# A two-layer attention and expert kernel: the first keys, the early jobs' transposes and the last gates are put in another order

## The chip, the cores and the metric

The kernel runs on one core of a Trainium2 chip. The metric is the device time of one execution in microseconds (us), lower is better. In what follows TensorE is called PE, VectorE DVE, ScalarE ACT, GpSimd POOL, and SyncE, which only starts DMAs here, SP. Each of these engines works through its own list of instructions in a fixed order, and an instruction that waits for another engine holds up everything behind it on its own list.

## The reference

Eight batches of 512 tokens with 256 features pass through two blocks. Each block is a layer norm, a cross-attention onto 64 context rows, and a feed-forward part, all with residuals.

```python
x = x + xattn0(layernorm(x), ctx)     # 16 heads of 16, 64 keys for each batch, biases on q, k, v, o
x = x + ffn0(layernorm(x))            # top 384 of 512 tokens: gelu(x @ w_block); the others pass through
x = x + xattn1(layernorm(x), ctx)     # the same with a mask
x = x + moe(x)                        # 8 experts, top 2 by softmax gate, weights made to sum to 1
                                      # expert: (silu(x @ g.T) * (x @ u.T)) @ down.T, 1024 hidden
```

Everything is float32. Layer norm has no learned scale. The expert part works on all 4096 tokens, each sent to two experts.

## The kernel before, in words

**Tiles.** A batch is four tiles of 128 tokens. Its residual rows stay in on-chip memory (`x_sb`). The context of all batches lies transposed in `ctxT`, so one pair of products with `wk` makes the keys of eight batches: `keys(l, c)` (L319 to L336) computes half c of layer l's keys and writes them twice, masked for the two heads of a pair by `headm`, into `kbd` (two DVE instructions at L332 for each half). `batch_values(b)` (L338 to L355) does the values of batch b for both layers and adds the bias `pre_b` while writing `vbd` (two DVE instructions at L353).

**The front stage.** For every batch a chain of steps is built: layer norm (statistics L385, `rstd` by POOL L390, `shift` L396, `xn` on ACT L399), transposes to `ps_x` (L414), queries (L446), scores `sc` (L476), the row maximum (L483), its transposes `pm` (L491), the transposed scores `st`, the context, the output product, then the ranked feed-forward part, the second attention, and the routing. Routing ends with `xr`, a token's row beside its expert and weight, which POOL scatters by indirect DMA into the table `xs` in device memory (L816). When half of the batches are scattered, seven "early" expert jobs of 256 tokens run between the steps of the other half (`early_steps`, L1066 to L1178): `enter` transposes the job's rows (L1111) and copies them on ACT (L1114), four `gates` steps do the gate and up products (L1135), and `down(0)` and `down(1)` do two output products (L1162), which POOL scatters with adding. Their weights come from SP in pieces of a single buffer set.

**The order.** The steps are laid out by a string, `ORDER` (L50 to L59). Each character takes the next step of one chain: a digit for a batch, A to H for the ranking of a batch, k for keys, v for `batch_values`, s for setups sorted by a number, l for the two lists of jobs, j for early jobs. `in_order` makes every step's instructions follow those of the step before it on PE, DVE, ACT and POOL. So the string is the order of the engines' queues in the front stage. DMAs on SP are not in it, but stand in program order with the ties named in the code.

**The late jobs.** After the front stage come 18 full jobs, 7 single and 11 paired ones, in the loop at L1443 to L1483. `load` (L1256) fetches a job's rows `xg` (L1277) and weights `wgu` (L1300), `wdn` on SP into four sets. `enter` (L1309) transposes the rows (L1317, ACT copy L1319), `gate_up_full` (L1340) makes the hidden rows (L1349), and `down` (L1396) the outputs, which POOL adds to `out_dram` (L106). A job's rows need every scatter of the front stage (`routed`). For the very first late job `load` issues the weights ahead of the rows (`late`), and its `enter` stands behind the last early job's outputs.

**Start.** `wk0`, half of batch 0's rows, `bk0`, `wv0` and `bq0` are on ACT's DMA queue, the context, the other rows and the remaining weights on SP's, and only the two value biases `bv0`, `bv1` on POOL's.

Of the kernel before, what the change touches and what calls it, by code (L numbers as in the profile page):

```python
# [8 lines left out]
F32 = mybir.dt.float32  # L9
I32 = mybir.dt.int32  # L10
# [37 lines left out]
NQ = P // QR  # L48

ORDER = """  # L50
sssssss0s0ksk0s1020001s0k110s1vs0s031010s7s2s40v320v2410030v20120ss01040502A010A30A0As10
1013010343201130005s12010sk0112151761Bs2B1BB112120241201v102s2050223s022302412C22123C2C0
21C02131012110323150030sv024110331231041025231052000043313234260000D14D34Ds14D2341v23361
3421632333442123454126154343114325134311114432E2524E1111544E452356E547224342372523465352
64345645256352452222F36F35F63F222246455635547335546357453674356647435356733333556646v7l6
3333476G464jj77j5jGj666j5j7jj47Gjjj765j7457j4G5j64654j7j6556747j5j7644644444j76sH6jj5644
44j557j76j7j57jj7Hsj76jjjjHH7565j65jj676jj7jj6j57j5j6j75557j5555jj7j6j667j55557jjjs67j66
j76j7676j66j76s66667j7jjjj7jj6666j77j7j7jjjjj77jjs7j7j7j7j7j777jj77jjjljj77jj77jj
"""  # L59


# [1 line left out]
def xattn_ffn_kernel(ctx: ExitStack, tc: tile.TileContext, a: dict, out: bass.AP):  # L63
# [28 lines left out]
    def after(i, others):  # L92
        for other in others:
            tc.add_manual_dep(
                i, other.name,
                mybir.DependencyInfo(mybir.DependencyClass.Sync, mybir.DependencyReason.DATA),
                reason="rows that it needs",
            )

    def apart(i, others, reason):  # L100
        for other in others:
            tc.declare_no_dep(i, other, reason=reason)
# [14 lines left out]
    with ExitStack() as front:  # L117
# [36 lines left out]
        def load_layer(l, names, q):  # L154
            for n in names:
                how = load_mat if n[0] == "w" else load_col if n in ("bk", "bq") else load_row
                layers[l][n] = how(q, f"{n}{l}")


        ctxT = pre[:, 0, :].rearrange("p (c b k) -> p c b k", c=2 * NC, b=B)[:, 0:NC]  # L160
        for c in range(NC):
            nc.sync.dma_start(
                ctxT[:, c].rearrange("p b k -> p (b k)"), a["ctxT"][c * P : (c + 1) * P, :]
            )
        load_layer(0, ("wk",), nc.scalar)
        for t in range(TB):
            q = (nc.scalar, nc.scalar, nc.sync, nc.sync)[t]
            q.dma_start(x_sb[:, t, :], x_t[0][:, t, :])
        load_layer(0, ("bk", "wv", "bq"), nc.scalar)
        load_layer(1, ("wv",), nc.sync)  # L170
        load_layer(0, ("wq", "bo", "wo"), nc.sync)
        nc.sync.dma_start(x_sb[:, TB : 2 * TB, :], x_t[1])
        load_layer(1, ("wk", "bk"), nc.sync)
        for b in range(2, 4):
            nc.sync.dma_start(x_sb[:, b * TB : (b + 1) * TB, :], x_t[b])
# [40 lines left out]
        def within(at, name, shape, bounds, lasts=False):  # L216
# [14 lines left out]
        every = slice(0, P)  # L231
        mhalf = const.tile([P, TB], F32, name="mhalf")
        setups.append((-0.9, lambda: nc.gpsimd.memset(mhalf, -0.5)))
        setups.append((
            -0.855, lambda: [load_layer(l, ("bv",), nc.gpsimd) for l in range(2)]
        ))

        ownh = within(
            -0.88, "ownh", [HC],
# [60 lines left out]
        mxs = []  # L300
        for i in range(3):
            mx = const.tile([P, TB, P], F32, name=f"mx{i}")
            setups.append(((-0.86, 0.25, 0.5)[i], lambda mx=mx: nc.vector.memset(mx, 0.0)))
            mxs.append(mx)
        turn = [0]

# [4 lines left out]
        vbd = const.tile([P, 2, B, NG, 2, DK], F32, name="vbd")  # L313
        for l in range(2):
            layers[l]["vbd"] = vbd[:, l]
        setups.append((
            -0.93, lambda: (nc.vector.memset(vbd[:, 0], 0.0), nc.gpsimd.memset(vbd[:, 1], 0.0)),
        ))

        def keys(l, c):  # L320
            w = layers[l]
# [727 lines left out]
        def part_of_room(*shape):  # L1049
            n = 1  # L1050
            for k in shape:
                n *= k
            v = room[:, took[0] : took[0] + n]
            took[0] += n
            names = " ".join("abc"[: len(shape)])
            return v.rearrange(f"p ({names}) -> p {names}", **dict(zip("abc", shape)))
# [2 lines left out]
        e_xg = part_of_room(2, RW)  # L1059
        e_xT = part_of_room(NC, 2, P)  # L1060
        e_sg = [part_of_room(1, 2 * P)]
        e_now = keep.tile([P, 2, D], F32, name="e_now")
        e_w = {}
        piece = 2 * P

# [118 lines left out]
        for b in range(B):  # L1184
# [2 lines left out]
                attention_steps(b, 0, layers[0], False) + ffn  # L1187
                + attention_steps(b, 2, layers[1], True) + route_steps(b)
            )
        chains["k"] = [lambda l=l, c=c: keys(l, c) for l in range(2) for c in range(NC)]  # L1190
        chains["v"] = [lambda b=b: batch_values(b) for b in range(B)]
        chains["s"] = [step for _, step in sorted(setups, key=lambda p: p[0])]
        chains["l"] = [early_list, full_list]
        chains["j"] = early = []
        jobs_steps = [early_steps(j) for j in range(NEARLY)]
        early += jobs_steps[0][0]
        for j, (_, steps) in enumerate(jobs_steps):

            loads = list(jobs_steps[j + 1][0]) if j + 1 < NEARLY else []
            for n, step in enumerate(steps):  # L1200
                early.append(step)
                if loads and n != len(steps) - 2:
                    early.append(loads.pop(0))


        engines = (
# [46 lines left out]
    def kind(j):  # L1253
        return "full" if j < NLATE else "one" if j < NLATE + NONE else "pair"

    def load(j, late=False):  # L1256

        what = kind(j)
        subs, n = (2 if what == "full" else 1), (2 if what == "pair" else 1)
        first = j if what != "pair" else NLATE + NONE + 2 * (j - NLATE - NONE)  # L1260
        size = P if what != "pair" else P // 2

        with tc.issue_after(last.pop().ins) if last else nullcontext():
            at = [
                (
                    nc.sync.value_load(
                        jobs[0:1, 0, u : u + 1], min_val=0, max_val=E * QROWS + P - subs * size
                    ),
                    nc.sync.value_load(jobs[0:1, 1, u : u + 1], min_val=0, max_val=E - 1),
                )  # L1270
                for u in range(first, first + n)
            ]
        xg = moe.tile([P, 2, RW], F32, tag="xg", name=f"xg_{j}", bufs=3)

        def rows():
            for u, (row, _) in enumerate(at):
                i = nc.sync.dma_start(  # L1277
                    xg[u * size : u * size + size, 0:subs, :],
                    xs[bass.ds(row, subs * size), :].rearrange("(s p) w -> p s w", p=size),
                ).ins  # L1280

                if what == "pair":
                    after(i, tail_sent)
                else:
                    for other in tail_sent:
                        tc.declare_no_dep(i, other, reason="rows of tokens alone")
                    after(i, routed)

        if not late:
            rows()  # L1290
        w = []
        for u in range(n):
            pool = wpool[sets[0] % 4]
            sets[0] += 1
            wgu = pool.tile([P, NC, 2 * FF], F32, tag="wgu", name=f"wgu_{j}_{u}")
            wdn = pool.tile([P, NF, D], F32, tag="wdn", name=f"wdn_{j}_{u}")
            w.append((wgu, wdn))
        for (_, e), (wgu, _) in zip(at, w):
            for c in range(NC):
                nc.sync.dma_start(  # L1300
                    wgu[:, c, :], gu_t[bass.ds(e, 1), :, c, :].rearrange("e p o -> (e p) o")
                )
        if late:
            rows()
        for (_, e), (_, wdn) in zip(at, w):
            i = nc.sync.dma_start(wdn, dn_t[bass.ds(e, 1), :, :, :].rearrange("e p f o -> (e p) f o"))
        last.append(i)
        return xg, w
# [127 lines left out]
    assert sorted(order) == [j for j in range(NJOB) if j != spare]  # L1436

    def load_at(i):
        return load(order[i], i == 0) if i < len(order) else None

    loads = [load_at(0), load_at(1)]
    entered = []
    in_order(lambda: entered.append(enter(order[0], loads[0][0])))  # L1443

    def placed(i, step):

        if i < NPIN:
            got = []
            in_order(lambda: got.append(step()))
            return got[0]  # L1450
        return step()

    pending = None
    for i, j in enumerate(order):
        w = loads.pop(0)[1]
        xT, tok, wt = entered.pop(0)
        if i > 0:
            loads.append(load_at(i + 2))
        if i == 0:

            hT = placed(i, lambda: gate_up_full(j, xT, w, None, range(NF // 2)))
            entered.append(placed(i, lambda: enter(order[1], loads[0][0])))
            placed(i, lambda: gate_up_full(j, xT, w, hT, range(NF // 2, NF)))
        elif j < NLATE:
            hT = placed(i, lambda: gate_up_full(j, xT, w))
        else:
            h, hT = placed(i, lambda: gate_up_rows(j, xT, w))
        if i == 0:
            small_list()
            unit_list()  # L1470
            loads.append(load_at(2))
        if 0 < i < len(order) - 1:
            entered.append(placed(i, lambda: enter(order[i + 1], loads[0][0])))
        if pending is not None:
            placed(i, lambda: down(*pending))
        if j >= NLATE:
            placed(i, lambda: turn(j, h, hT))
        pending = (j, hT, w, tok, wt)
# [55 lines left out]
```

## Time and profile before

| what | value |
|---|---|
| time, median of 3 runs | 1164.99 us (1164.78 to 1166.47) |
| profiled execution, its own time | 1173.17 us |
| profiled execution, span from first to last instruction | 1171.5 us |
| mean granted PE clock in it | 0.998 of full |
| PE busy | 1146.6 us, 98% of the span |
| DVE / ACT / POOL busy | 574.6 / 372.9 / 283.5 us |
| data moved by DMA | 203.53 MB |

The time of a run is that of the whole execution; the span counts from the core's first to its last instruction in the profile. All durations below come from the one profiled execution, which took 8.2 us more than the median of the runs. In rows of the timeline the first number is the start in us from the span's start, the second the time to the end of the group, then engine, line, operation, result and operands, shape, and in brackets how long the engine had been idle before and what ended the wait.

### The profile page before, as it was taken

How to read it: one execution, taken by the hardware profiler on the slowest of the kernel's cores; microseconds unless marked ns; L12 is line 12 of the kernel's file. 1: busy time of each engine (PE TensorE's matmuls, PEld its weight loads, DVE VectorE, ACT ScalarE, POOL GpSimd, SP SyncE). 2: the span in 40 equal slices, each digit the busy share in tenths (PEclk: the TensorE clock that was granted, in tenths of full speed). 3: DMA queues.
4: the chain of work that ended last, by engine and by line, in shares of the span. 5: the costliest groups of instructions: out<-in, count | busy, mean ns of one | idle time of the engine just before them, and what ended most of it. 6: DMA issues, size and time to landing. Idle time of an engine off the chain costs nothing. (4 is left out here: it accounts for less than half of the span.)

```text
span 1171.5 us, 20900 instructions
## 1 busy us (share of the span) xinstructions
PE 1146.6 (98%) x8010; PEld 825.0 (70%) x8010; DVE 574.6 (49%) x1664; ACT 372.9 (32%) x713; POOL 283.5 (24%) x307
## 2 busy tenths in 40 slices
PE   7999999999999999999999999999999999999997
PEld 3565666656657777778787876777767777677786
DVE  6898888878878676556722221221212222222211
ACT  3655645645543433232121121221111211112210
POOL 5331134123440411431412112112121121211212
PEclk9999999999999999999999999999999999999999
DMA  9000001010125344445789688896889967987711
GB/s 270 2 1 2 1 20 38 19 56 20 38 86 165 105 138 115 136 145 163 207 329 353 237 295 293 303 312 224 288 290 330 312 214 272 314 309 237 279 14 19
DMA packets 119988, 203.53 MB, mean 174 GB/s; under 512 B 10608, under 2 KB 105712, under 8 KB 108368
## 3 DMA queue, kind: packets, MB, share of 16 engines
q1 hardware_dynamic: 100048, 179.35, 43.5%
q0 software_dynamic: 14496, 17.86, 7.5%
q10 hardware_dynamic: 5344, 4.98, 1.3%
q8 instruction: 64, 1.05, 0.4%
q14 instruction: 36, 0.29, 0.1%
HBM read 180.38 MB, written 23.47 MB: 174 GB/s over the span
## 5 line engine op out<-in xcount | busy, mean ns | idle before, releaser
L1349 PE MATMUL gu<-xjT,wgu 128*128 128x256 f32 x1152 | 252.0, 379 | 0.7 <-ACT xjT L1319 0.7
L1349 PEld LDWEIGHTS gu<-xjT,wgu 128*128 128x128 f32 x1152 | 217.6, 190 | 31.0 <-issue 1.2
L106 POOL DMA_INDIRECT out_dram<-now,tok x63 | 98.5, 1564 | 474.6 <-DVE now L1414 296.4
L1406 PE MATMUL o<-wdn,hT 128*128 128x256 f32 (+1 forms) x1008 | 189.2, 380 | 0.0
L1406 PEld LDWEIGHTS o<-wdn,hT 128*128 128x128 f32 (+1 forms) x1008 | 151.1, 173 | 28.3 <-issue 1.7
L1358 DVE TENSOR_TENSOR hT<-sg,gu 128x256 f32<-128x256 f32 x144 | 60.6, 421 | 190.6 <-ACT sg L1357 186.7
L1357 ACT ACTIVATE sg<-gu 128x256 f32<-128x256 f32 x144 | 55.3, 384 | 208.5 <-PE gu L1349 205.7
L1376 PE MATMUL gr<-wgu,xjT 128*64 128x512 f32 (+1 forms) x432 | 120.8, 596 | 0.0
L1135 PE MATMUL gu_e<-x_sb,e_wgu 128*128 128x256 f32 x448 | 101.8, 382 | 0.8 <-ACT x_sb L1114 0.6
L1135 PEld LDWEIGHTS gu_e<-x_sb,e_wgu 128*128 128x128 f32 x448 | 83.8, 190 | 15.9 <-issue 2.8
L1414 DVE TENSOR_SCALAR now<-o,wt 128x256 f32<-128x256 f32 x53 | 25.6, 483 | 137.1 <-PE o L1406 137.1
L1376 PEld LDWEIGHTS gr<-wgu,xjT 128*64 128x64 f32 (+1 forms) x432 | 42.8, 150 | 68.4 <-issue 67.0
L390 POOL TENSOR_TENSOR rstd<-ve,mhalf 128x4 f32<-128x4 f32 x32 | 33.0, 1031 | 233.0 <-DVE ve L388 185.4
L816 POOL DMA_INDIRECT xs<-xr,slots x64 | 63.3, 989 | 105.0 <-issue 35.3
L483 DVE TENSOR_REDUCE mx<-sc 128x32 f32<-128x2048 f32 x32 | 73.2, 2287 | 21.4 <-PE sc L476 17.9
L1386 DVE TENSOR_TENSOR h<-sg,gr 128x512 f32<-128x512 f32 x34 | 23.4, 687 | 83.5 <-PE gr L1376 83.4
L446 PE MATMUL ps_q<-xT,w_wq 128*128 128x512 f32 x128 | 62.0, 612 | 0.5 <-ACT xT L417 0.5
L577 PE MATMUL py<-w_wo,cT 128*128 128x256 f32 x256 | 60.3, 384 | 0.0
L1385 ACT ACTIVATE sg<-gr 128x512 f32<-128x512 f32 x34 | 20.3, 597 | 124.7 <-PE gr L1376 124.7
L577 PEld LDWEIGHTS py<-w_wo,cT 128*128 128x128 f32 x256 | 47.3, 190 | 11.7 <-issue 5.3
L399 ACT ACTIVATE xn<-x_sb,shift,rstd 128x256 f32<-128x256 f32 x96 | 49.8, 594 | 17.9 <-DVE shift L396 16.6
L385 DVE BATCH_NORM_STATS2 st<-x_sb 128x6 f32<-128x256 f32 x128 | 51.3, 401 | 4.9 <-DMA x_sb<-in_x_dram 4.8
(286 smaller groups left out, 1455.8 us busy)
## 6 DMA issues: line engine op xcount, KB each, us to landing
wgu<-in_guT_dram SPq DMA_DIRECT2D x90, 1024.0 KB
wdn<-in_dnT_dram SPq DMA_DIRECT2D x45, 1024.0 KB
e_wgu<-in_guT_dram SPq DMA_DIRECT2D x56, 256.0 KB
e_wdn<-in_dnT_dram SPq DMA_DIRECT2D x7, 1024.0 KB
xg<-xs SPq DMA_DIRECT2D x18, 260.0 KB
out_dram<-x_sb ACTq DMA_DIRECT2D x8, 512.0 KB
x_sb<-in_x_dram SPq DMA_DIRECT2D x7, 512.0 KB
x_sb<-xs SPq DMA_DIRECT2D x7, 260.0 KB
```

The source lines that it names most:

```text
L106: i = nc.gpsimd.indirect_dma_start(out=out_rows, out_offset=bass.IndirectOffsetOnAxis(ap=tok, axis=0), in_=rows, in_offset=None, bounds_ch ...
L385: nc.vector.bn_stats(st, x_sb[:, b * TB + t, :])
L446: nc.tensor.matmul(ps, lhsT=w["wq"][:, k, c * P : (c + 1) * P], rhs=got["xT"][:, k, :], start=(k == 0), stop=(k == NC - 1),)
L483: nc.vector.tensor_reduce(got["mx"].rearrange("p t (r h) -> p r t h", r=NQ)[:, :, :, 2 * c : 2 * c + 2], sc, AX.X, ALU.max,)
L577: nc.tensor.matmul(py[:, s, :], lhsT=cT[:, c, t * P : (t + 1) * P], rhs=w["wo"][:, c, :], start=(c == 0), stop=(c == NC - 1),)
L816: i = nc.gpsimd.indirect_dma_start(out=xs, out_offset=bass.IndirectOffsetOnAxis(ap=slots[:, t, k : k + 1], axis=0), in_=xr[:, t, :], in_of ...
L1135: nc.tensor.matmul(ps[:, half, :], lhsT=e_w["gu"][:, c, o : o + P], rhs=e_xT[:, c].rearrange("p s q -> p (s q)"), start=(c == 0), stop=(c ...
L1349: nc.tensor.matmul(ps[:, half, :], lhsT=wgu[:, c, o : o + P], rhs=xT[:, c].rearrange("p s q -> p (s q)"), start=(c == 0), stop=(c == NC - 1),)
L1357: nc.scalar.activation(sg[:, 0 : 2 * P], ps[:, 0, :], AF.Silu)
L1358: nc.vector.tensor_tensor(hT[:, f, :], sg[:, 0 : 2 * P], ps[:, 1, :], ALU.mult)
L1376: nc.tensor.matmul(ps[rows], lhsT=xT[:, c, 0, rows], rhs=wgu[:, c, o : o + 4 * P], start=(c == 0), stop=(c == NC - 1),)
L1406: nc.tensor.matmul(ps[rows], lhsT=hT[:, f, s * P + rows.start : s * P + rows.stop], rhs=wdn[:, f, :], start=(f == 0), stop=(f == NF - 1),)
```

## The change

It has four parts.

*Head.* A new setup `run_up` issues three products of zeros (128x256, operands from `mx0`, whose memset becomes DVE's first). `wk0` is loaded in two halves. `first_keys` replaces both `keys(0, c)`: it takes both output halves through the first half of `wk0`, then both through the second. The four writes of `kbd` move from DVE to ACT as activations with scale `headm` and a bias `bkh`, which two new POOL instructions make from `bk0`; on ACT's queue they stand ahead of batch 0's `xn`. `batch_values` of batches 1 to 3 move from between later steps to the place ahead of the first transposes. `bk0`, `wv1` and `bq0` go to POOL's DMA queue beside `bv0`, `bv1`; `wv0`, `wq0` and batch 1's rows move up on SP's queue ahead of `bo0`, `wo0`.

*Early jobs.* The `enter` of job j+1 moves from behind `down(0)` and `down(1)` of job j to the place ahead of them.

*From early to late jobs.* The rows of the first late job are loaded by `first_rows`, ahead of its weights on SP; `first_enter` transposes them ahead of `down(0)` of the last early job. In `ORDER` the scatters of the last batches stand earlier: `s20`, `s21` (batch 7, tile 2) ahead of `down` of job 5, and `s30`, `s31` ahead of the first gates of job 6. `load` loses its `late` form.

*End.* In the last full job the gates are parted in two halves, with the pending `down` of the job before between them.

The core of the diff (the string `ORDER` changes in its first and last lines only as told above):

```diff
-sssssss0s0ksk0s1020001s0k110s1vs0s031010s7s2s40v320v2410030v20120ss01040502A010A30A0As10
+sssssssssss0k0vvv0ss1020001s0k110s1s0s031010s7s2s403202410030v20120ss01040502A010A30A0As
...
+        layers[0]["wk"] = pre_w[:, pre_at["wk0"]]
-        load_layer(0, ("wk",), nc.scalar)
+            nc.scalar.dma_start(layers[0]["wk"][:, c, :], a["wk0"][c * P : (c + 1) * P, :])
-        load_layer(0, ("bk", "wv", "bq"), nc.scalar)
-        load_layer(1, ("wv",), nc.sync)
-        load_layer(0, ("wq", "bo", "wo"), nc.sync)
+        load_layer(0, ("wv", "wq"), nc.sync)
         nc.sync.dma_start(x_sb[:, TB : 2 * TB, :], x_t[1])
+        load_layer(0, ("bo", "wo"), nc.sync)
...
+            load_layer(0, ("bk",), nc.gpsimd)
+            load_layer(1, ("wv",), nc.gpsimd)
+        setups.append((-0.862, loaded))
+            for l in range(2):
+                load_layer(l, ("bv",), nc.gpsimd)
+            load_layer(0, ("bq",), nc.gpsimd)
+        setups.append((-0.855, loaded))
...
+        def run_up():
+            ps = ps_m.tile([P, S], F32, tag="m", name="ps_w")
+            for _ in range(3):
+                nc.tensor.matmul(
+                    ps[:, 0 : 2 * P],
+                    lhsT=mxs[0][:, 0, :],
+                    rhs=mxs[0][:, 0:2, :].rearrange("p t k -> p (t k)"),
+                    start=True,
+                    stop=True,
+                )
+        setups.append((-0.95, run_up))
...
+        def first_keys():
+            w = layers[0]
+            two = [ps_m.tile([P, B, SK], F32, tag="m", name=f"ps_k_0_{c}") for c in range(NC)]
+            for i in range(2):
+                nc.gpsimd.tensor_scalar(
+                    bkh[:, i, :], w["bk"], headm[:, i : i + 1], None, ALU.mult
+                )
+            for k in range(NC):
+                for c in range(NC):
+                    nc.tensor.matmul(two[c], lhsT=w["wk"][:, k, c * P : (c + 1) * P],
+                        rhs=ctxT[:, k], start=(k == 0), stop=(k == NC - 1))
+            for c in range(NC):
+                for i in range(2):
+                    nc.scalar.activation(
+                        w["kbd"][:, c, :, i, :], two[c], AF.Identity,
+                        bias=bkh[:, i, c : c + 1], scale=headm[:, i : i + 1],
+                    )
...
+        def first_rows():
+            with tc.issue_after(last.pop().ins):
+                first_at.append((...))
+            i = nc.sync.dma_start(
+                e_xg, xs[bass.ds(first_at[0][0], 2 * P), :].rearrange("(s p) w -> p s w", p=P)
+            ).ins
+            last.append(i)
+            after(i, routed)
+        def first_enter():
+            ps = ps_m.tile([P, NC, 2, P], F32, tag="m", name="ps_e_first")
+            for c in range(NC):
+                for k in range(2):
+                    nc.tensor.transpose(ps[:, c, k, :], e_xg[:, k, c * P : (c + 1) * P], ident)
+            nc.scalar.copy(first_xT, ps)
...
-            for n, step in enumerate(steps):
+            for n, step in enumerate(steps[1:-2]):
+                if loads:
+                    early.append(loads.pop(0))
+                elif n == 0:
+                    step = lambda step=step: (first_rows(), step())
                 early.append(step)
-                if loads and n != len(steps) - 2:
-                    early.append(loads.pop(0))
+            if loads:
+                early.append(loads.pop(0))
+                early.append(jobs_steps[j + 1][1][0])
+                early += steps[-2:] + loads
+            else:
+                early += [lambda step=steps[-2]: (first_enter(), step()), steps[-1]]
...
-    in_order(lambda: entered.append(enter(order[0], loads[0][0])))
+    entered = [(first_xT, first_tok, first_wt)]
...
+        elif i == len(order) - 1 and j < NLATE:
+            hT = gate_up_full(j, xT, w, None, range(NF // 2))
+            down(*pending)
+            pending = None
+            gate_up_full(j, xT, w, hT, range(NF // 2, NF))
```

## The prediction

> **What bounds the kernel now.** I read the page first, then waits, windows and timeline around each edit.
>
> ```profile
> PE 1146.6 (98%) x8010; PEld 825.0 (70%) x8010; DVE 574.6 (49%) x1664; ACT 372.9 (32%) x713; POOL 283.5 (24%) x307
> ...
> PE   7999999999999999999999999999999999999997
> ```
>
> PE is busy 1146.6 of 1171.5 us. The change takes no product out and adds three small ones, so it can only touch the 24.9 us in which PE idles: 5.15 before the first product, some 7 in the end, and small waits between. I ask at each edit which PE wait goes and which one comes.
>
> **Head.** Batch 0's and batch 1's way to PE before:
>
> ```profile
> 8.88 1.04 POOL L390 TENSOR_TENSOR rstd<-ve,mhalf 128x4 f32<-128x4 f32 x1 [5.15 <-DVE ve L388]
> ...
> 9.90 1.38 POOL L149 DMA_DIRECT2D pre_b<-in_bv_dram  x2
> ...
> 10.16 2.08 ACT L399 ACTIVATE xn<-x_sb,shift,rstd 128x256 f32<-128x256 f32 x4 [2.11 <-DVE shift L396]
> ...
> 15.31 0.69 ACT L453 ACTIVATE qT<-ps_q,c_bq 128x512 f32<-128x512 f32 x1 [1.59 <-PE ps_q L446]
> ...
> 18.11 0.43 DVE L385 BATCH_NORM_STATS2 st<-x_sb 128x6 f32<-128x256 f32 x1 [1.52 <-DMA x_sb<-in_x_dram]
> ...
> 21.06 2.23 DVE L483 TENSOR_REDUCE mx<-sc 128x32 f32<-128x2048 f32 x1
> ...
> 21.30 0.33 PE L414 MATMUL ps_x<-ident,xn 128*128 128x128 f32 x1 [1.29 <-ACT xn L399]
> ```
>
> Batch 0's scores end at 18.09, but DVE reaches their maximum only at 21.06: it first does batch 2's statistics, whose rows land at 18.11. So batch 0 has about 3 us of slack before. The change spends it. `bkh` stands behind `rstd` on POOL, which ends at 9.92. No row of before shows this instruction; the nearest is POOL's TENSOR_SCALAR of 128x1, 0.83 us (L908). Two end at 11.6, the first at 10.75. Then ACT writes `kbd` four times; I price each as the ACT activation of 128x512 from PSUM, 0.69 (L453 above), 2.76 in all. Batch 0's `xn`, behind them on ACT, starts at T = 13.9 instead of 10.16 (12.9 if a `bkh` costs 0.2, 14.5 if POOL's DMA issues ahead of it hold `rstd` by 0.5).
>
> From there I keep PE's durations of before: batch 0's scores end at T+7.9, batch 1's transposes stand at T+10.9 without their 1.29 wait, the second maximum ends at T+14.5, and `pm` comes at T+14.55 = 28.45, where it was at 28.91. The two break even at T = 14.36. Values 2 and 3 are also gone from the later stretch, worth 0.55 there, since one of them stood where PE had to wait. Sum about -1.0 for T = 13.9, about -1.8 for T = 12.9.
>
> Against it stands the clock.
>
> ```profile
> 20.00:30.00 10.00, 8.25 (x61) 5.04 (x64) 7.74 (x11) 4.33 (x8) 7.40 (x13) 0.83 0.87 257
> ```
>
> The eighth number is the granted clock: 0.83 over 10 us, half speed for some 3.4 us, after a thin stretch. The Trainium skill ("TensorE: Matmul & The Clock Gate", "What's actually happening") says that the gate closes after an idle window of about 3.4 us and opens after as long a busy one. By that rule the three products of zeros, at the 0.86 us that a cold pass of the keys took, fill 2.6 us and need not open it. The sum is the same either way: the keys end at 8.6 or 10.6, ahead of T. But the rule speaks against the later T: PE has little between the last values and 14.5, and a closed gate over the queries would cost up to 1.7 of which 0.7 is absorbed, so +1.0. I weigh this in: head -0.7, from -1.8 to +1.0. DVE's lost `kbd` writes (4 of 1.53) lie beside other work and are covered by the wait for batch 2's rows.
>
> **Early jobs.** `enter` ahead of `down` takes cover from whatever follows `enter`. At most places nothing is late there: the maximum or the reciprocal that comes next has ended under the products of the attention. There I cost it at nothing; uncovered, each would cost up to 2.3. The exception is batch 7's last maximum:
>
> ```profile
> 491.60 2.29 DVE L483 TENSOR_REDUCE mx<-sc 128x32 f32<-128x2048 f32 x1 [0.28 <-PE sc L476]
> 492.04 3.32 PEld L1162 LDWEIGHTS o_e<-e_wdn,x_sb 128*128 128x128 f32 x16 [0.20 <-issue]
> 492.04 3.72 PE L1162 MATMUL o_e<-e_wdn,x_sb 128*128 128x256 f32 x16
> ...
> 495.60 0.60 PE L491 MATMUL pm<-ident,mx 128*128 128x128 f32 x4
> ```
>
> The output products of job 3 cover the maximum. Afterwards `enter` of job 4 (0.6) stands there, and `pm` waits from 492.6 to about 494.0: +1.4 (0.5 to 1.7). The output products, ready all along, are queued behind `pm`.
>
> **From early to late jobs.**
>
> ```profile
> 557.33 1.05 POOL L816 DMA_INDIRECT xs<-xr,slots  x1 [20.92 <-issue]
> ...
> 559.40 0.91 PE L1135 MATMUL gu_e<-x_sb,e_wgu 128*128 128x256 f32 x3 [0.61 <-ACT x_sb L1114]
> ...
> 567.01 0.91 SPq L1300 DMA_DIRECT2D wgu<-in_guT_dram  x2
> ...
> 575.66 0.96 POOL L816 DMA_INDIRECT xs<-xr,slots  x1 [0.30 <-issue]
> ...
> 578.62 0.39 SPq L1277 DMA_DIRECT2D xg<-xs  x1
> ...
> 581.67 0.63 PE L1317 MATMUL ps_x<-ident,xg 128*128 128x128 f32 x4 [0.79 <-DMA xg<-xs]
> ...
> 582.97 1.35 PE L1349 MATMUL gu<-xjT,wgu 128*128 128x256 f32 x5 [0.68 <-ACT xjT L1319]
> ```
>
> Before, the last scatter is held in the queue until 575.66. 2.0 us after its end the rows are issued, and 3.05 later PE has them. PE pays 0.79 + 0.68 here, and 0.61 for ACT ahead of job 6's gates. Moving `enter` of job 6 ahead of job 5's outputs (7.07 us) hides the 0.61, less some 0.15 that job 5's end then shows: gates of job 6 end at 573.0 instead of 573.46.
>
> The scatters then run at POOL's own pace. From 557.33, six at a pitch of 1.29 and two adding ones of job 5 at 1.93 reach 568.9, and two more end at 571.2. Rows are issued 2.0 later, at 573.2, and reach PE at 576.2. PE has nothing else from 573.0, because `first_enter` stands ahead of job 6's outputs: a wait of 3.2. Then transposes 0.6 and outputs 7.07, under which the ACT copy hides; the first late products start at 583.9 instead of 582.97: +0.9 (0.4 to 1.2). On SP the weights of the first late job now stand behind these rows. They were issued at 567.01, and landed complete 8.9 later; from 573.8 they land near 582.7, 1.2 ahead of need. Everything later is carried over: the weight sets behind are prefetched well ahead.
>
> **End.**
>
> ```profile
> 1163.27 1.56 POOL L106 DMA_INDIRECT out_dram<-now,tok  x1 [3.61 <-issue]
> ...
> 1165.13 1.56 POOL L106 DMA_INDIRECT out_dram<-now,tok  x1 [0.30 <-DVEq L1483]
> ```
>
> The last but one scatter waits 3.61, its rows being ready at 1161.3; freed, it ends early and the last one starts when its own rows are scaled, at 1165.0: -0.1. Parting the gates reorders the same products, and the hidden rows' 1.3 us latency is covered by outputs of 7 us.
>
> **Sum.** -0.7 + 1.4 + 0.9 - 0.1 = +1.5 us, against the profiled execution's 1173.17 (span 1171.5). The median of runs is 8.2 lower; the head, the seam and the end are waits of fixed size, so I carry the +1.5 over: 1164.99 + 1.5 = 1166.5. Own range of this case +/-2.
>
> **Rivals.**
>
> *Slower: late biases at the head.* DVE's six `vbd` adds of values 1 to 3 (0.43 each, 2.6) now stand ahead of `c_bq`'s scaling and batch 1's statistics, and wait for `bv0`, `bv1`, which POOL issues. In before these took from 9.90 to 17.8, 7.9 us, with the DMA engines full (share 1.00 from 10 to 20). The Trainium skill ("DMA: Bandwidth & Descriptors", "Anatomy of one DMA — SWDGE (gpsimd) path") fits a POOL-issued transfer by 2.0 us plus bytes over 436 GB/s, about 2.3 for 128 KB. Issued near 6, they land at 8.3 by the page and 13.9 by the row. DVE must begin the adds by 12.8 to be done with batch 1 (2.4) when batch 2 lands at 18.1; every us later is one lost. By the page it costs nothing; by the row 1.1; with a landing at 17.8 as before, 5.0. I take 12.5, nearer the row as the queues are less full at 6, hence nothing in the sum. This case decides from 14 on and gives +3 to +6.5, 1169.5 in the middle. Chance 0.25.
>
> *Faster.* `bkh` is cheap (T = 12.9: head -1.8), the maximum of batch 7 finds cover, and the rows are routed by 570, in which case both waits at the seam go (-1.5 with the gates' 0.45). Total about -3, 1162.0. For it: POOL's pitch contains 0.3 of issue, and small POOL instructions of the setup cost 0.1 to 0.5. Against it: the adding scatters stand between the last ones. Chance 0.17.
>
> *The rest* is the main case, 0.58. About a quarter of it (0.14) lies over 0.2% slower.
>
> **Numbers.** 0.2%, 2.3 us, is about what a measurement of this kernel can tell from no change. Faster 0.17; slower 0.25 + 0.14 = 0.39; within 0.44. The range 1162.5 to 1170.5 leaves out half of the faster case and the dearest third of the slower one. The main case alone is 1164.5 to 1168.5.
>
> **What would show it.** Right: `xn` of batch 0 near 13.9 with `pm` at 28 to 28.5; a PE wait of 1.4 for `mx` behind job 4's `enter`; a wait near 3 ahead of the first rows' transposes, none at the ACT copy; first late products about 1 us later relative to job 5's gates. Wrong: DVE idle for `pre_b` over 1 us ahead of batch 1's statistics, a granted clock below 0.8 between 10 and 30, a PE wait for `wgu` at the first late job, or rows landing before job 6's gates end.

## The result, and the profile after

The changed kernel takes 1171.11 us (median of 7 runs, 1169.94 to 1174.7) against 1165.24 us for the kernel before (7 runs, 1164.78 to 1167.04). The ratio is 1.0052 with a 95% interval of 1.0041 to 1.0064: slower by 0.52%, some 6 us, where +1.5 us and a range up to 1170.5 were forecast.

The two profiled executions hide this: 1173.17 us before, 1172.83 after. The profile of before was the odd one (experiment 1 settles it), so the reading has to go by stages, not by spans. The table has the length of each stage from PE's rows. *Head*: start to batch 0's first output product `py`. *45 to 360*: from there to the last `py` ahead of the early jobs' outputs (367.81 before). *Jobs*: from there to the last ranking product `pc` (547.39). *Seam*: from there to the transposes of the second late job (589.98). *Late*: from there to PE's last product. *End*: what the span has after it. All in us:

| kernel | head | 45 to 360 | jobs | seam | late | end |
|---|---|---|---|---|---|---|
| before, first profile | 44.43 | 323.38 | 179.58 | 42.60 | 574.22 | 7.3 |
| before, second profile (e1) | 42.89 | 317.54 | 178.65 | 42.33 | 574.22 | 7.5 |
| after | 45.45 | 317.30 | 182.64 | 44.13 | 574.21 | 7.4 |
| e2, head alone | 43.94 | 317.41 | 178.91 | 42.60 | 574.22 | 7.4 |
| e3, `enter` alone | 42.27 | 317.34 | 182.32 | 42.26 | 574.22 | 7.4 |
| e4, seam alone | 44.49 | 317.44 | 179.03 | 45.60 | 574.21 | 7.4 |
| e7, after, `enter` back | 43.20 | 317.35 | 179.14 | 44.34 | 574.21 | 7.4 |

The first profile of before was 6 us longer in a stretch that the change does not touch. Against the second one the changed kernel lost 2.6 in the head, 4.0 in the jobs and 1.8 at the seam, and got nothing at the end. That is more than the 6 us between the medians, because these two executions are not the middle ones: the changed kernel's took 1172.83 us and the second one of before 1164.80. The head is where executions differ most: e7 has the same head as the changed kernel, at 43.20.

The head of the changed kernel, from the timeline:

```profile
10.76 1.05 POOL L438 TENSOR_TENSOR rstd<-ve,mhalf 128x4 f32<-128x4 f32 x1 [3.90 <-DVE ve L436]
11.82 0.56 POOL L349 TENSOR_SCALAR bkh<-c_bk,headm 128x2 f32<-128x2 f32 x2
...
12.15 2.79 ACT L363 ACTIVATE kbd<-ps_k,bkh,headm 128x512 f32<-128x512 f32 x4 [7.94 <-POOL bkh L349]
...
12.70 1.75 DVE L401 TENSOR_TENSOR vbd<-ps_v,pre_b 64x256 f32<-64x256 f32 x4 [0.69 <-DMA pre_b<-in_bv_dram]
...
14.82 2.07 ACT L447 ACTIVATE xn<-x_sb,shift,rstd 128x256 f32<-128x256 f32 x4
...
15.53 2.75 PE L462 MATMUL ps_x<-ident,xn 128*128 128x128 f32 x8
...
18.10 4.94 PE L494 MATMUL ps_q<-xT,w_wq 128*128 128x512 f32 x8
```

The chain is the one that was forecast: `rstd`, `bkh`, four writes of `kbd`, and only then `xn`, at 14.82 instead of 13.9. The biases landed at 12.7. But the queries took 4.94 us, where before they took 3.70:

```profile
13.29 3.70 PE L446 MATMUL ps_q<-xT,w_wq 128*128 128x512 f32 x8 [0.24 <-ACT xT L417]
```

The windows of the changed kernel say why (eighth number, granted clock; read in narrower windows it is 0.50 from 13.80 to 20.63):

```profile
10.00:20.00 10.00, 7.64 (x33) 3.60 (x29) 6.60 (x25) 5.91 (x10) 4.49 (x9) 0.69 0.97 298
20.00:30.00 10.00, 9.94 (x87) 5.32 (x85) 7.38 (x12) 4.43 (x9) 7.49 (x14) 0.97 0.86 256
```

The early jobs have three PE waits that before did not have, one of them foreseen:

```profile
378.83 1.14 PE L462 MATMUL ps_x<-ident,xn 128*128 128x128 f32 x8 [0.50 <-ACT x_sb L1200]
...
457.10 1.13 PE L1248 MATMUL o_e<-e_wdn,x_sb 128*128 128x256 f32 x4 [0.87 <-DVE e_now L1256]
...
487.94 2.29 DVE L531 TENSOR_REDUCE mx<-sc 128x32 f32<-128x2048 f32 x1 [0.28 <-PE sc L524]
...
488.38 0.66 PE L1197 MATMUL ps_e<-ident,x_sb 128*128 128x128 f32 x4
...
490.29 0.66 PE L539 MATMUL pm<-ident,mx 128*128 128x128 f32 x4 [1.25 <-DVE mx L531]
```

The last is the uncovered maximum, 1.25 where 1.4 was said. The first two end not with data but with the emptying of a buffer in PSUM, the memory that PE writes its results to: ACT's copy of the `enter` before (L1200), and DVE's scaling of the first output (L1256). And the seam, the stretch from the early to the late jobs:

```profile
550.02 7.17 PE L1248 MATMUL o_e<-e_wdn,x_sb 128*128 128x256 f32 x32 [0.25 <-DVE x_sb L1231]
...
571.34 0.38 SPq L1125 DMA_DIRECT2D x_sb<-xs  x1
...
574.27 0.63 PE L1137 MATMUL ps_e_first<-ident,x_sb 128*128 128x128 f32 x4 [2.49 <-DVE x_sb L1230]
...
574.74 7.07 PE L1248 MATMUL o_e<-e_wdn,x_sb 128*128 128x256 f32 x32
...
581.85 0.48 DVE L1256 TENSOR_SCALAR e_now<-o_e,wt_e 128x256 f32<-128x256 f32 x1 [0.87 <-PE o_e L1248]
582.54 1.75 PE L1437 MATMUL gu<-x_sb,wgu 128*128 128x256 f32 x7 [0.73 <-issue]
```

PE stands 2.49 us with the outputs queued behind the transposes. The trace names a DVE instruction, but the transposes read the rows that SP sent for at 571.34; at the same place in e8 and e10 it names these rows (`DMA x_sb<-xs`). Then the first late products wait 0.73 again. The wait goes to "issue", but in e4, e8, e10 and e12, which have the same products at that place, the trace names DVE's `e_now`: the last output must leave PSUM first.

### The profile page after: what moved, and what is told of

Its sections match the earlier page's. It is cut to its first block, busy times and chain, and to the rows that moved or that the text cites. A ratio compares the mean times of both kernels' runs of the same rounds, so it can differ in the third digit from the quotient of the medians.

```text
span 1171.1 us, 20926 instructions
## 1 busy us (share of the span) xinstructions
PE 1147.8 (98%) x8016; PEld 825.1 (70%) x8016; DVE 571.0 (49%) x1660; ACT 375.4 (32%) x717; POOL 285.0 (24%) x312
## 3 DMA queue, kind: packets, MB, share of 16 engines
q8 instruction: 64, 1.05, 0.4%
## 5 line engine op out<-in xcount | busy, mean ns | idle before, releaser
L1437 PE MATMUL gu<-xjT,wgu 128*128 128x256 f32 x1088 | 238.1, 379 | 0.0
L1437 PEld LDWEIGHTS gu<-xjT,wgu 128*128 128x128 f32 x1088 | 205.6, 190 | 28.5 <-issue 1.2
L106 POOL DMA_INDIRECT out_dram<-now,tok x61 | 94.9, 1556 | 450.8 <-DVE now L1502 311.4
```

What stands on the lines that cost most here:

```text
L106: i = nc.gpsimd.indirect_dma_start(out=out_rows, out_offset=bass.IndirectOffsetOnAxis(ap=tok, axis=0), in_=rows, in_offset=None, bounds_ch ...
L1437: nc.tensor.matmul(ps[:, half, :], lhsT=wgu[:, c, o : o + P], rhs=xT[:, c].rearrange("p s q -> p (s q)"), start=(c == 0), stop=(c == NC - 1),)
```

## The experiments

**e1, the kernel of before once more.** No edit.

> The kernel of before, unchanged (one empty line more). Its one profiled execution took 1173.17 us, 8 us over its median, and stood 5.7 us behind the changed kernel's profile between 205 and 347 us, a stretch that the change does not touch. Theory A: that was a disturbance of this one execution; a second profile has a span near 1163 to 1165 and the stretch 205 to 347 is some 6 us shorter, so the two profiles compare wrongly there and the change costs about 6 us elsewhere. Theory B (rival): the changed kernel really gains 5 to 6 us there, through the way its head shifts batch 1 against batch 0, and loses 11 us in other places; then the second profile of before looks like the first, span near 1171.

1164.48 us (18 runs, 1163.78 to 1166.94) against 1165.22 for before on the same chips, ratio 0.9992 (0.9985 to 0.9999); span 1163.1. The same kernel thus differs from itself by 0.08%, and a difference of that size between two kernels says nothing. The stretch from 45 to 360 has 317.54 us, as in the other kernels run beside it. So the first profile was disturbed there, and the changed kernel gains nothing in it: theory A. Why DVE and PE ran later there was not found. The clock of the head differs too: the second profile has none of the closed window that the first had at 20 to 30.

```profile
20.00:30.00 10.00, 8.44 (x74) 4.30 (x74) 9.00 (x14) 4.42 (x8) 7.40 (x13) 1.00 0.83 246
```

With it `pm` of batch 0 came 1.5 us earlier than in the first profile, which the prediction measured against; first the row of the first profile, then that of e1:

```profile
28.92 0.66 PE L491 MATMUL pm<-ident,mx 128*128 128x128 f32 x4
...
27.37 0.65 PE L492 MATMUL pm<-ident,mx 128*128 128x128 f32 x4
```

**e2, head alone.** All of the change's head in the kernel of before.

> The kernel of before with the head of the change alone (zero products, keys by halves on ACT, values in front of the first transposes, loads moved). Theory A (the PE clock closes over batch 0's late transposes and queries, in one or two windows of 3.4 us depending on where the window falls): +1.0 to +3.0 us, with a granted clock of 0.5 for 3.4 to 6.8 us between 10 and 21 us and times that spread by some 2 us. Theory B (prediction's own sum): -0.7 us. Theory C: the head does nothing that lasts, within 0.3 us.

1166.86 us (14 runs, 1164.59 to 1168.47) against 1165.22, ratio 1.0006 (0.9997 to 1.0014). The profile has `py` 1.05 later than e1. `xn` starts at 13.60, near the forecast, and then:

```profile
14.31 0.77 PE L462 MATMUL ps_x<-ident,xn 128*128 128x128 f32 x2 [0.79 <-ACT xn L447]
...
16.87 4.65 PE L494 MATMUL ps_q<-xT,w_wq 128*128 128x512 f32 x8
...
28.93 0.66 PE L539 MATMUL pm<-ident,mx 128*128 128x128 f32 x4 [0.50 <-DVE mx L531]
```

```profile
10.00:20.00 10.00, 6.90 (x27) 3.37 (x24) 6.92 (x25) 6.06 (x11) 4.11 (x9) 0.83 0.98 297
```

The queries take 4.65 instead of 3.70, in a window with the clock at 0.83 (closed from 15.40 to 18.81). The gain of 0.7 does not show; a loss of about 1 us is what the profile has, though the interval of the times still reaches zero.

One profile cannot say how often the clock closes here. The head of before has a closed window between 20 and 30 in four of its eight profiles (the first one, e4, e9, e10), the head of the change one between 13 and 21 in three of four (the changed kernel, e2, and e6 without the zeros, but not e7). The mean granted clock, on record for every run, says it without a profile: 0.9961 over the 14 runs here, 0.9974 over the 44 of before beside them (single runs of both lie between 0.995 and 0.999). Over 1165 us this is 1.5 us more at which the clock was not granted, no less than the whole difference of the times.

**e3, `enter` alone.** Transposes of jobs 1 to 6 ahead of the outputs before them.

```diff
-            for n, step in enumerate(steps):
-                early.append(step)
-                if loads and n != len(steps) - 2:
+            for step in steps[1:-2]:
+                if loads:
                     early.append(loads.pop(0))
-
+                early.append(step)
+            if loads:
+                early.append(loads.pop(0))
+                early.append(jobs_steps[j + 1][1][0])
+            early += steps[-2:] + loads
```

> The kernel of before with the transposes of early jobs 1 to 6 ahead of the outputs of the job before, nothing else. Theory A (the outputs were the cover of three waits: the next transposes of batch 6 at job 1, the second outputs of job 2, the maximum at job 4; 0.5 + 0.9 + 1.25, less the 0.6 hidden at job 6 and what the old places cost): +2 to +3 us. Theory B (prediction's own sum: job 4 alone): +1.4 less 0.45, about +1.0. Theory C: the waits only move and PE catches up later: 0.

1168.58 us (13 runs) against 1165.22, ratio 1.0026 (1.0018 to 1.0035): +3.0. The jobs stage is 182.32 against 178.65, with the same three waits of 0.50, 0.87 and 1.25 as in the changed kernel. The waits count PE's idle time alone. Product by product against e1, PE falls back by 0.90, 1.13 and 1.80 us at these three places and nowhere else in the stage (changed kernel against e7: 0.90, 1.13, 1.64). Theory A.

**e4, seam alone.** `first_rows`, `first_enter` and the end of `ORDER` in the kernel of before, jobs' `enter` behind the outputs, the last gates not parted.

> The kernel of before with the first late job's rows loaded ahead of its weights and transposed ahead of the last early job's outputs, and the last scatters placed earlier; the transposes of jobs 1 to 6 stay behind the outputs. Theory A: a PE wait near 2.5 us ahead of the first rows' transposes and 0.7 for the weights after the outputs, 0.8 + 0.7 removed: +1.0 to +1.7 us (0.6 for ACT ahead of job 6's gates stays). Theory B: rows arrive in time and the seam gains: -1.5.

1167.39 us (11 runs, 1165.14 to 1170.24) against 1165.22, ratio 1.0017 (1.0005 to 1.0028): +2.0. The waits are those expected, 2.48 and 0.78. But the seam is 45.60, 3.3 more than in e1, and the reason is new:

```profile
565.00:570.00 5.00, 2.52 (x13) 1.97 (x12) 4.89 (x24) 1.15 (x3) 0.00 (x0) 0.97 0.56 170
570.00:575.00 5.00, 5.00 (x19) 4.19 (x18) 1.84 (x12) 0.59 (x1) 0.00 (x0) 0.68 0.98 388
```

```profile
569.57 0.94 PE L1089 MATMUL ps_e_first<-ident,x_sb 128*128 128x128 f32 x4 [2.48 <-DVE x_sb L1182]
570.31 8.48 PE L1200 MATMUL o_e<-e_wdn,x_sb 128*128 128x256 f32 x32
```

Behind the wait of 2.5 us the clock gate closed, and the outputs took 8.48 us instead of 7.07. So the price of the wait was here itself plus 1.4. The profiled execution, 1169.86 us, is one of five with a mean clock of 0.995, which took 1168.76 to 1170.24; the other six, at 0.997 to 0.999, took 1165.14 to 1167.39. The median of +2.0 lies between the two kinds.

**e5, head with the keys first.** One character of `ORDER` moves.

```diff
-sssssssssss0k0vvv0ss1020001s0k...
+sssssssssssk00vvv0ss1020001s0k...
```

> The head of the change alone, with one step moved: the keys stand ahead of batch 0's statistics in the order, so that the two small POOL instructions for the scaled bias come ahead of rstd and ACT can write kbd as soon as the keys are done. In the head alone kbd began at 10.9, after rstd and the biases, and batch 0's xn at 13.6, with PE waits of 1.9 and 0.8 us ahead of its transposes. Theory A (the place of these two instructions made xn late, and PE idle enough for a closed gate): kbd begins near 8.5, xn near 11.5 to 12.3, the two PE waits shrink below 1 us together, the clock closes less often, and the time is 1 to 2 us below the head alone: -0.5 to -1.0 us against before. Theory B (the head loses by late input rows and by values in front): no better than the head alone, +0.7 to +1.6 us.

1164.68 us (13 runs) against 1165.21, ratio 0.9996 (0.9988 to 1.0005).

```profile
7.39 0.57 POOL L349 TENSOR_SCALAR bkh<-c_bk,headm 128x2 f32<-128x2 f32 x2 [0.56 <-DMA c_bk<-in_bk_dram]
...
8.27 2.79 ACT L363 ACTIVATE kbd<-ps_k,bkh,headm 128x512 f32<-128x512 f32 x4 [4.05 <-PE ps_k L354]
...
11.06 2.07 ACT L447 ACTIVATE xn<-x_sb,shift,rstd 128x256 f32<-128x256 f32 x4
...
14.13 2.19 DVE L401 TENSOR_TENSOR vbd<-ps_v,pre_b 64x256 f32<-64x256 f32 x5 [3.10 <-DMA pre_b<-in_bv_dram]
...
15.13 1.06 PE L462 MATMUL ps_x<-ident,xn 128*128 128x128 f32 x8 [2.21 <-DVE vbd L401]
```

`kbd` and `xn` come as early as theory A says. Yet PE's transposes wait just as long, now for a PSUM buffer that holds values until the biases land at 14.13. In this profile, which has a closed clock window too (16.30 to 19.71), `py` stands at 44.16, no better than e2. The ratio is 0.10% below e2's, 1.2 us, each taken against before on its own chips, and the intervals overlap: inconclusive on the time, clear on the next limit.

**e6, head without the products of zeros.** `run_up` is not issued.

> The head of the change alone without the three products of zeros. Theory A (they are too short to open the clock for good and end long ahead of the transposes): within 0.5 us of the head alone, +0.7 to +1.6 us against before. Theory B (they keep the clock open over the keys and values and this carries over): 1 to 2 us slower than the head alone.

1166.33 us (13 runs) against 1165.21, ratio 1.0003 (0.9994 to 1.0011). No difference from e2 (1.0006) that these runs can tell, so no worth of the zeros shows here.

**e7, the changed kernel with `enter` of jobs 1 to 5 put back.**

> The changed kernel with the transposes of early jobs 1 to 5 put back behind the outputs of the job before (job 6 stays ahead of them). Theory A (the outputs were the cover of three waits of 0.5, 0.9 and 1.25 us): these waits are gone and the time is some 3.0 us below the changed kernel, near 1168, +2.7 us against before. Theory B (prediction: the maximum of batch 7 alone): 1.4 below, near 1169.7.

1167.91 us (22 runs) against 1165.21, ratio 1.0022 (1.0015 to 1.0029), which leaves some 2.6 of the changed kernel's 6 us. The jobs stage is back to 179.14. In the trace the maximum is covered again:

```profile
483.90 2.29 DVE L531 TENSOR_REDUCE mx<-sc 128x32 f32<-128x2048 f32 x1 [0.28 <-PE sc L524]
...
484.33 3.72 PE L1248 MATMUL o_e<-e_wdn,x_sb 128*128 128x256 f32 x16
...
487.89 0.60 PE L539 MATMUL pm<-ident,mx 128*128 128x128 f32 x4
```

**e8, a seam meant to be better.** Weights first on SP, rows on ACT's queue behind the last gates, transposes between the last two outputs, job 6's `enter` ahead (lines against the changed kernel).

```diff
-            i = nc.sync.dma_start(
-                e_xg, xs[bass.ds(first_at[0][0], 2 * P), :].rearrange("(s p) w -> p s w", p=P)
+            row = nc.scalar.value_load(
+                jobs[0:1, 0, 0:1], min_val=0, max_val=E * QROWS + P - 2 * P
+            )
+            i = nc.scalar.dma_start(
+                e_xg, xs[bass.ds(row, 2 * P), :].rearrange("(s p) w -> p s w", p=P)
...
-                early += [lambda step=steps[-2]: (first_enter(), step()), steps[-1]]
+                early.append(lambda step=steps[-2]: (first_rows(), step(), first_enter()))
+                early.append(steps[-1])
```

> The kernel of before with another seam: last scatters early as in the change, the first late job's weights ahead of everything on SP as in before, its rows loaded on ACT's DMA queue behind the last gates, transposed between the two outputs of the last early job, and job 6's transposes ahead of job 5's outputs. Theory A (the seam lost because PE stood at the transposes with the outputs queued behind, and the weights stood behind the rows on SP): no PE wait over 0.3 us between job 5's and the first late products, -1.5 to -2.0 us against before. Theory B (the weights or rows cannot come earlier for want of DMA bandwidth): a wait of 1 us or more remains, -0.5 to +0.5.

1172.50 us (6 runs) against 1165.21, ratio 1.006 (1.0047 to 1.0073): 7 us lost, not 2 won. ACT issued the rows at 570.11, 2.8 us after its last gate, and PE waited 4.87:

```profile
574.00 1.11 PE L1083 MATMUL ps_e_first<-ident,x_sb 128*128 128x128 f32 x4 [4.87 <-DMA x_sb<-xs]
```

My first reading, that ACT's reading of the row number cost this, was tested by e10. This trace already speaks against it: SP, which waited for the scatters, sent for the next job's rows at 570.09, at the same moment.

**e9, the least of the seam.** Last scatters early, job 6's `enter` ahead, gates parted; rows, weights and transposes of the first late job as in before.

> The kernel of before with the least of the seam: last scatters early as in the change, job 6's transposes ahead of job 5's outputs, last gates parted; the first late job's weights, rows and transposes stay where they were in before. Theory (rows come by 570 under the outputs of job 6, so the wait for them goes, and ACT's copy ahead of job 6's gates is hidden; ACT's copy ahead of the first late products stays, 0.7): -0.5 for the rows, -0.35 for job 6, -0.3 at the end, together -1.0 to -1.2 us against before. Rival (early scatters delay what POOL does after them, or the rows wait for something else): 0 to +1.

1165.61 us (13 runs, 1163.34 to 1169.75) against 1166.40, ratio 0.9999 (0.9989 to 1.0009). No gain, and the seam at 42.79 is no shorter. The last scatter was issued by 567.65, yet SP sent the rows only at 575.20. SP's waits and the summary of the scatters' line:

```profile
SPq L1284 <- DMA xs<-xr,slots: 10.6, 1, 10.6
```

```profile
DMA to landing us min/median/max: 2.4/2.8/9.2
```

SP waited for the scatters themselves. In e4, where the weights stand behind the rows, the same summary has a maximum of 5.4:

```profile
DMA to landing us min/median/max: 2.4/2.7/5.4
```

**e10, the rows on POOL's queue** right behind the last scatter, everything else as in e8, gates parted.

```diff
-            row = nc.scalar.value_load(
+            row = nc.gpsimd.value_load(
...
-            i = nc.scalar.dma_start(
+            i = nc.gpsimd.dma_start(
```

> As the better seam that lost 7 us, but the first late job's rows are loaded on POOL's DMA queue right behind the last scatter, where POOL has nothing to do, instead of on ACT's behind the last gates; last gates parted too. There ACT issued the rows 2.8 us after its last gate because it first had to read the row number from memory, and PE waited 4.9 us. Theory A (that read, on ACT's busiest path, was the loss): rows land before job 6's first output is done, no PE wait at the transposes, -1.0 to -1.6 us against before (the first late products still wait 0.7 for DVE to empty the last output). Theory B (rows behind the scatters cannot land before 572 whatever the queue): PE waits 3 us or more, +2 us or worse.

1177.52 us (4 runs) against 1166.40, ratio 1.0101 (1.0085 to 1.0116). POOL ended its last scatter at 565.43 and then stood before the rows:

```profile
573.82 0.78 POOL L1072 DMA_DIRECT2D x_sb<-xs  x1 [8.39 <-issue]
```

PE waited 9.36, and the clock was closed from 573.67 to 583.91. So reading the row number on ACT was not the main cause. The scatters took up to 9.4 us to land here, 8.3 in e8 and 9.2 in e9, all with the first late job's weights issued ahead; with the rows ahead of the weights (the changed kernel, e4, e7) 5.8, 5.4 and 4.7. The rows wait for the last scatter, so theory B holds.

**e11, e10 with the head of the change, keys first and values in their old places.**

> The kernel before this one in the list with the head of the change, keys first in the order, and the batch values in their old places, so that PE does not wait for the value biases, which landed at 14.1 when the keys stood first. Theory A (batch 2's rows, landing near 18, set the head whatever stands before, so the head cannot gain): within 0.5 us of the kernel without this head. Theory B (keys first and values late is a better head): 1 us faster than without it, -2 to -2.5 us against before.

1174.83 us (5 runs) against 1166.40, ratio 1.0082 (1.0069 to 1.0096). That is 2.7 us below e10 by medians of few runs, of which the profiles put 0.9 at the seam. Its py at 43.37 came with two closed clock windows at 11.6 to 18.4, against 45.02 in e10 with one; so a head of this kind may be worth 1 to 2 us, but this pair with its disturbed seam is too rough to say so.

**e12, the change's order on SP with the transposes between the two outputs,** the head of before, job 6's `enter` alone ahead.

> The head of before, job 6's transposes alone ahead of job 5's outputs, and the seam of the change (last scatters early, rows ahead of the weights on SP, last gates parted) with one step moved: the first late job's transposes stand between the two outputs of job 6 instead of ahead of both. Theory A (the outputs queued behind the transposes were the seam's loss; scatters land in time only while no weights stream): the PE wait of 2.5 us ahead of the transposes falls below 0.5 us, the first late products wait for the weights or the last output's bank by 0.7 to 2 us, and the time is -0.5 to -1.5 us against before. Theory B (the weights behind the rows on SP then set the start of the first late job): the wait moves there whole, 2.5 us or more, 0 to +1.5 us against before.

1171.46 us (13 runs) against 1171.71 (17 runs), ratio 1.0001 (0.9991 to 1.0012). In these runs both kernels took some 6 us longer, e12 in the stretch from 45 to 360 (323.47, as in the first profile of before), so only the ratio counts. The wait ahead of the transposes is gone, but the first late products wait 0.78 for the last output's buffer and then 1.15 for the weights, and behind these two waits the clock closed:

```profile
579.23 0.67 PE L1389 MATMUL gu<-x_sb,wgu 128*128 128x256 f32 x2 [0.78 <-DVE e_now L1208]
581.05 8.43 PE L1389 MATMUL gu<-x_sb,wgu 128*128 128x256 f32 x30 [1.15 <-DMA wgu<-in_guT_dram]
```

```profile
581.94:585.35 3.41, 3.41 (x10) 2.66 (x9) 0.42 (x1) 1.67 (x2) 0.00 (x0) 0.50 1.08 401
```

The seam is 44.86, of which the half clock took about 1.7. The gain expected by theory A did not come. Of the 2.5 us of wait 1.15 moved to the weights, which is the place that B names but not the whole wait that it expects. No version tried beats the kernel of before by more than the runs can tell.

## Why the prediction was wrong, point by point

**The sum.** Forecast -0.7 + 1.4 + 0.9 - 0.1. Measured alone: head +0.7 (ratio 1.0006), `enter` +3.0 (1.0026), seam +2.0 (1.0017), together 5.7 against 6.1 for the whole. So the parts add within their intervals (0.1% each way), and every term but the end erred to the same side.

**Head: the failing step was "-0.7".** T was right in its mechanism and, by luck, nearly in its size (13.60 alone, 14.82 in the changed kernel), because two errors cancelled: a `bkh` cost 0.28, not 0.83, but batch 0's rows, and with them `rstd`, came later than before (9.55 and 10.76 instead of 8.88). What failed is the comparison behind T. With e2's T of 13.60 the sum T+14.55 puts `pm` at 28.15, which less the mark of 28.91 and the 0.55 of the later stretch is -1.3; e2 against e1 shows +1.05. The larger share, 1.5, is the mark: it held a closed window of its own, which e1 lacks. The other 0.8 came behind T, where I kept the PE durations of before and took a closed clock only as an upper bound; e2 has `pm` at 28.93. The 0.55 came as 0.51. The rule of the Trainium skill on the clock ("TensorE: Matmul & The Clock Gate", "What's actually happening"), that an idle window of about 3.4 us closes it, pointed the right way, though here a window did not have to be wholly idle: in e2 PE worked 1.9 of the 3.4 us ahead of the closed stretch. (Two slips that move nothing: the fast end, T = 12.9, adds to -2.0 and not -1.8, and DVE's `kbd` writes took 1.53 for two, not each.)

**Early jobs: "there I cost it at nothing" was the largest miss.** The named wait (1.4) came as 1.25. Two others, of 0.50 behind job 1's `enter` and of 0.87 at job 2's second output behind job 3's `enter`, came where I had looked only at whether the next operand is ready. Both are PSUM buffers, of which the pool has four that go round. An `enter` takes one, which is held until ACT, busy with `ex` and `xn`, copies it; the fifth user, batch 6's transposes, waits for that copy. Between job 2's two outputs stand two groups of transposes and a ranking product, so the second output needs the buffer of the first, which DVE empties only at 456.57, behind other work. Together 2.62 us of wait and 3.7 in PE's starts, and e3 and e7 show the 3 us both ways.

**Seam: the failing step was "none at the ACT copy".** Counted from the last ranking product, the rows came as forecast: PE began their transposes 28.88 us behind it (574.27 less 545.39), the prediction's sum gives 28.8 (576.2 less 547.39). The wait was 2.49 and not 3.2 because job 6's gates ended later than forecast. The 0.61 ahead of them went, but 0.25 and 0.28 stand in its place, and they end 26.39 us behind the ranking product (571.78) where before they ended 26.22 behind it (573.61): the 0.45 was not gained. That cost nothing, since PE waits for the rows anyway. What the sum lacks is the wait behind the outputs: ACT's 0.68 is hidden, but 0.73 for the PSUM buffer of the last output took its place. So the first late products start 1.6 us later than in the first profile of before, where 0.9 was forecast, and 1.8 later than in e1, whose rows came 0.3 sooner. The weights were in time, as said, in the changed kernel.

**End: -0.1 or nothing.** The stage after PE's last product is 7.4 against 7.3 and 7.5, and 7.0 to 7.5 in e9 to e12, which part the gates too.

**The rival "late biases".** They landed at 12.7, close to the 12.5 that I took, and below the point from which that case decides. With the keys first (e5) they land at 14.1 and do hold PE. The fit of the Trainium skill ("DMA: Bandwidth & Descriptors", "Anatomy of one DMA — SWDGE (gpsimd) path"), by estimate about 2.3 us for such a transfer, would have them landed by 8.6 (issued from 5.2 to 6.3); with the DMA engines 0.97 busy from 10 to 20 the row of before was the nearer guide.

## What to carry to other kernels

When a step is moved on the PE queue, count its PSUM buffer as well as its operands: who empties it, what stands ahead of that copy on the emptying engine, and which product needs the buffer next. A PE wait of 2 to 3 us can cost more than its length, because the clock gate may close behind it (2.48 us of wait and 1.4 of slow products in e4). And a mark for "before" should come from more than one profile: one execution here was 6 us long in a stretch that nothing had touched, and 1.5 us late in the head.

## What the runs showed of the hardware that I had not expected

An indirect scatter's landing time depends on what else is on the DMA engines: at median 2.6 to 2.8 us, but at most 6.9 to 9.4 in the seven profiles with the first late job's weights (3 MB on SP's queue) issued ahead of the last scatters, and at most 4.7 to 5.8 in the three with them behind. In this kernel the chain "scatter, then read back" wants bulk loads behind it.

The clock gate closed in e4 after a wait of 2.48 us between two full stretches of products; the changed kernel's profile has a wait of 2.49 at the same place and a full clock. The closed stretches say what decides. Each one ahead of the end of the run has a granted clock of 0.5 and lasts 3.41 us or a multiple of it (6.83 in the changed kernel's head, 10.24 in e10), and two in one execution start a whole number of such windows apart: 23.61 and 569.75 in e4 are 160 apart, 24.13 and 573.67 in e10 161. So the windows lie on a grid, at another place in each execution. In e4 the wait lay within one window (first row; the first busy time is PE's), and the next one was closed:

```profile
566.34:569.75 3.41, 0.93 (x6) 0.53 (x5) 3.33 (x15) 0.77 (x2) 0.00 (x0) 1.00 0.65 186
569.75:573.16 3.41, 3.41 (x11) 2.84 (x10) 2.09 (x12) 0.59 (x1) 0.00 (x0) 0.50 0.98 406
```

In the changed kernel, with the grid counted on from its closing at 13.80, the wait lay across a border, and the clock stayed open; so it did in e7 with a wait of 2.70 (2.09 and 2.03 us of work):

```profile
570.17:573.58 3.41, 1.61 (x8) 1.08 (x6) 3.30 (x18) 0.98 (x3) 0.00 (x0) 1.00 0.38 93
573.58:576.99 3.41, 2.72 (x15) 2.49 (x16) 2.60 (x13) 0.76 (x2) 0.00 (x0) 1.00 0.98 393
```

Every closing between 5 and 1100 us in these profiles followed a window in which PE worked 0 to 2.0 us. Not every such window closed the gate, as the 1.61 above shows, so a limit cannot be read from these runs.
